# A three-layer graph network: attribute loads ten steps earlier, and early-row products in two PSUM banks

## Chip, core and metric

The kernel runs on one core of a Trainium2 chip. The metric is the device time of one execution in microseconds (us), the median of several runs. The engines are TensorE (PE, with its weight loads shown as PEld), VectorE (DVE), ScalarE (ACT), GpSimd (POOL) and the queue engine SyncE (SP). DMAs are issued from SP, ACT and POOL.

## What is computed

A relational graph convolution over 6250 nodes with 256 features and 100,000 edges with 32 attributes each, three layers deep, and a layer norm at the end. The edges come sorted by destination. Everything is float32.

```python
ew = edge_attr @ edge_w + edge_b                       # [100000, 256]
inv_cnt = [1 / max(segment_sum(edge_type == i, dst), 1) for i in range(3)]
x0 = x
for l in range(3):
    msg = relu(x[src] * ew)                            # gather of 100000 rows
    out = 0
    for i in range(3):
        h = segment_sum(msg * (edge_type == i), dst) * inv_cnt[i]
        out = out + h @ weights[l, i]
    x = x + relu(out + x @ roots[l] + biases[l])
return layernorm(x0 + x)
```

## The kernel before

**Pairs, quads and steps.** The edges are cut into 782 tiles of 128. Two tiles are a *pair* (391 of them, `U`), two pairs share one buffer `xs` and are called a *quad* here. Each layer walks over the pairs in an order written out by hand (`schedule`): first pairs 64 to 390, then 63 down to 0. So the edges of the lowest nodes, the first 128 rows above all, come last in a layer. The walk is a loop over steps `it`; in step `it` each kind of work handles the pair that lies some distance ahead or behind, and the instructions are issued in exactly this order on each engine (`manual_schedule`, no reordering).

**One quad's way through the engines.**
- POOL gathers its rows, four indirect DMAs of 128 rows (helper at L928), nine steps ahead of the reduction.
- PE multiplies the edge attributes by `edge_w` (`make_ew`, L623, PSUM tile `ew_p`, three banks, of which a quad takes two).
- DVE multiplies the two (`weigh`, two instructions, L645), ACT applies the relu (`bound`, L649), DVE makes one-hot matrices of the destinations (`one_hot`, L655).
- PE reduces the edges onto their destinations (`reduce`, L665, PSUM tile `h_p`), eight instructions to a pair in layers 1 and 2 and ten in layer 0. DVE adds the result into a ring `acc` (`add`, L683).

When all edges of a block of 128 nodes are in, `node_mul` (L711) and `node_end` (L742 to L745) finish the block's rows in `x_all`, and SP stores them to `x_mid[l]` in DRAM (L747), where the next layer gathers from. Block 0 is the last of a layer.

**The ring of row buffers.** `xs` has eight buffers (`ROWS`), three of which stay with the first three quads of layer 0 (`first_rows`, made ahead of the layers). Five rotate: the gathers of a quad wait until the quad five places before it has been reduced.

**Across a layer's end.** The first six pairs of the next layer, three quads, are gathered early (`gather_early`, L806), while block 0 isn't finished. In `x_mid` block 0 is zero until its store, so these quads lack what the first 128 rows contribute. `complete` (L634 to L639) puts it in: for each of a quad's two pairs PE multiplies `came`, a one-hot matrix of the sources below 128, with block 0 of `x_all`, and DVE adds the product to the pair's rows. The product of a pair fills the PSUM tile `o_p`, which has one bank (`o_pool`, `bufs=1`) and serves `node_mul` too. `r_p` (`r_pool`) is another tile of one bank; `root_turn` and `root_mul` use it (L688, L696) and, for blocks 0 and 1, the second half of `node_mul`. The store of block 0 waits for the twelve early gathers, which read `x_mid`; the gathers after them wait for that store.

**The attributes.** In layer 0 the attributes are loaded in their plain form (L536), turned by PE (L607), copied to the tile `at` by ACT (`keep_attrs`, L615) and kept in DRAM as `at_all` by SP (`store_at`, L599), eight pairs (512 KB) at a time. Layers 1 and 2 load `at` from there (`load_at`, L563). `at` has three buffers. The first two groups of the next layer are loaded by the layer before, at steps `U` and `U + 1` (`ats_next`), and handed on; the other loads come nine steps ahead of their use. In SP's queue these two loads stand behind the next layer's `r_sb` and `b_sb` (L552, L554, step `U - 10`). In layer 0 the last `store_at`, step `U - 5`, stands ahead of them too; the store of block 0 stands behind them.

Of the kernel before, what the change touches and what calls it, by code (L numbers as in the profile page):

```python
# [8 lines left out]
F32 = mybir.dt.float32  # L9
# [433 lines left out]
def ordered_path(ctx, tc, x, edge_attr, weights, roots, biases, edge_w, edge_b, out, src, src_i, seg, place_i, consts, rows,  # L443
# [7 lines left out]
    P = 128  # L451
    N, D = x.shape
    E, A = edge_attr.shape
    L, R = weights.shape[:2]
# [3 lines left out]
    U = T // 2  # L458
# [59 lines left out]
    o_pool = ctx.enter_context(tc.tile_pool(name="o_p", bufs=1, space=PSUM))  # L518
    r_pool = ctx.enter_context(tc.tile_pool(name="r_p", bufs=1, space=PSUM))

    groups = list(dict.fromkeys(u // 4 for u in order))
    at_groups = list(dict.fromkeys(u // GROUP for u in order))

    def first_of(p, n):
        return p == 0 or order[p - 1] // n != order[p] // n
# [4 lines left out]
    def load_attrs(g):  # L530

        an = ans[groups.index(g) % 3]
        t0 = 8 * g
        full = min(8, E // P - t0)
        if full > 0:
            nc.sync.dma_start(an.rearrange("p k i a -> p (k i) a")[:, :full, :A],  # L536
                              edge_attr[t0 * P:(t0 + full) * P, :].rearrange("(g p) a -> p g a", p=P))
        if 0 <= full < 8 and (t0 + full) * P < E:
            nc.sync.dma_start(an.rearrange("p k i a -> p (k i) a")[:E - (t0 + full) * P, full, :A],
                              edge_attr[(t0 + full) * P:, :])  # L540

    def load_x(c0):
        n = min(6, NT - 1 - c0)
        if n > 0:
            nc.scalar.dma_start(x_all[:, c0:c0 + n, :], x[c0 * P:(c0 + n) * P, :].rearrange("(c p) d -> p c d", p=P))
        if c0 + 6 >= NT - 1:
            last = N - (NT - 1) * P
            nc.scalar.dma_start(x_all[:last, NT - 1, :], x[N - last:, :])

    def load_root(l):  # L550
        r_sb = wpool.tile([P, DC, D], F32, name="r_sb")
        nc.sync.dma_start(r_sb, roots[l].rearrange("(c p) e -> p c e", p=P))  # L552
        b_sb = wpool.tile([P, D], F32, name="b_sb")
        nc.sync.dma_start(b_sb, biases[l:l + 1, :].to_broadcast([P, D]))  # L554
        return r_sb, b_sb

    def pairs_in(g):
        return min(GROUP, U - GROUP * g)

    def load_at(l, g):  # L560
        at = edge.tile([P, GROUP, P], F32, name="at", bufs=3)
        if l > 0:
            nc.sync.dma_start(at[:, :pairs_in(g)].rearrange("p k e -> p (k e)"), at_all[g, :, :pairs_in(g) * P])  # L563
        return at

    def find_came():
        e = 2 * P * order[0]
        nc.scalar.dma_start(came_i.rearrange("p t e -> p (t e)"),
                            src[e:e + 2 * FIRST * P][None, :].to_broadcast([P, 2 * FIRST * P]))
        for t in range(2 * FIRST):  # L570
            nc.vector.tensor_scalar(came[:, t, :], came_i[:, t, :], node_i[:, 0:1], None, op0=ALU.is_equal)

    def layer(l, r_sb, b_sb, ats, early, pools):
# [13 lines left out]
        r_next, ats_next, early_next = (None, None), {}, {}  # L587

        def gather(u):
            p = order.index(u)  # L590
            if p < FIRST:
                xs[u // 2] = early[u // 2]
            else:
                if first_of(p, 2):
                    xs[u // 2] = room(rows, D)
                gather_pair(nc, xs[u // 2], x_rows, src_i, u)
# [4 lines left out]
        def pairs_of(q):  # L601
            return range(min(2, U - 2 * q))
# [24 lines left out]
        def gather_early(p):  # L627
            u = order[p]
            if first_of(p, 2):
                early_next[u // 2] = room(rows, D)  # L630
            gather_pair(nc, early_next[u // 2], x_mid[l], src_i, u)

        def complete(q):
            for k in pairs_of(q):  # L634
                rest = o_pool.tile([P, 2, D], F32, name="o_p")
                for i in range(2):
                    nc.tensor.matmul(rest[:, i, :], came[:, 4 * q + 2 * k + i - 2 * order[0], :], x_all[:, 0, :],  # L637
                                     start=True, stop=True)
                nc.vector.tensor_add(xs[q][:, k], rest, xs[q][:, k])  # L639

        def weigh(q):
            n = len(pairs_of(q))
            for i in (1, 0):
                there = xs[q][:, :n, i, :]
                nc.vector.tensor_mul(there, ew_ps[q][i][:, :n, :], there)  # L645

        def bound(q):
            there = xs[q][:, :len(pairs_of(q))]
            nc.scalar.activation(there, there, AF.Relu)  # L649
# [116 lines left out]
        def load_x0(c):  # L766
            n = min(P, N - c * P)
            x0s[c] = edge.tile([P, D], F32, name="x0", bufs=2)
            if n < P:
                nc.vector.memset(x0s[c], 0.0)  # L770
            nc.sync.dma_start(x0s[c][:n, :], x[c * P:c * P + n, :])
# [12 lines left out]
        for it in range(-11, max(starts) + 7):  # L784
            def pair(k):
                return order[it + k] if 0 <= it + k < U else None
            if pair(AHEAD) is not None:
                gather(pair(AHEAD))
            if l < L - 1 and 0 <= it + AHEAD - U < FIRST:
                gather_early(it + AHEAD - U)  # L790
            if l == 0 and it == 20:
                find_came()
            if l == 0 and pair(11) is not None and first_of(it + 11, 4):
                load_attrs(pair(11) // 4)
            if l > 0 and pair(AHEAD) is not None and pair(AHEAD) // GROUP not in ats:
                ats[pair(AHEAD) // GROUP] = load_at(l, pair(AHEAD) // GROUP)
            if l == 0 and it >= -4 and (it + 4) % 20 == 0 and (it + 4) // 20 * 6 < NT - 1:
                load_x((it + 4) // 20 * 6)
            if it == 10:
                nc.sync.dma_start(w_sb, weights[l].rearrange("r (c p) e -> p (r c) e", p=P))  # L800
            if l == L - 1 and it + 2 in root_at:
                load_x0(root_at[it + 2])
            if l < L - 1 and it == U - 10:
                r_next = load_root(l + 1)
            if l < L - 1 and U <= it < U + 2:
                ats_next[at_groups[it - U]] = load_at(l + 1, at_groups[it - U])  # L806

            if pair(4) is not None and first_of(it + 4, 2):
                make_ew(pair(4) // 2)
            if pair(0) is not None:  # L810
                reduce(pair(0))
            if pair(-LAG) is not None:
                add(pair(-LAG))
            if pair(3) is not None and first_of(it + 3, 2):
                if l > 0 and it + 3 < FIRST:
                    complete(pair(3) // 2)
                weigh(pair(3) // 2)
                bound(pair(3) // 2)
            if l == 0:

                for k, work in ((6, keep_attrs), (7, turn)):
                    if pair(k) is not None and first_of(it + k, 2):
                        work(pair(k) // 2)
                if pair(4) is not None and last_of(it + 4, GROUP):
                    store_at(pair(4) // GROUP)
            if it in root_at:
                root_turn(root_at[it])
            if it - 1 in root_at:
                root_turned(root_at[it - 1])
            if it - 2 in root_at:  # L830
                root_mul(root_at[it - 2])
            if it - 3 in root_at:
                root_keep(root_at[it - 3])
            if it == moved:
                move()
            if it - 2 == moved:
                clear(P)
            if it + 1 in node_at and slot_of(node_at[it + 1]) == 0:
                wrap()
            if it in node_at:  # L840
                node_mul(node_at[it], 0)
            if it - 1 in node_at:
                node_end(node_at[it - 1], 0)
            if it - 2 in node_at:
                node_mul(node_at[it - 2], 1)
            if it - 3 in node_at:
                node_end(node_at[it - 3], 1)
                clear(slot_of(node_at[it - 3]))
            if it - 4 in node_at and l == L - 1:
                deviate(node_at[it - 4])  # L850
            if it - 5 in node_at and l == L - 1:
                norm(node_at[it - 5])
            if pair(2) is not None and first_of(it + 2, 2):
                one_hot(pair(2) // 2)
# [248 lines left out]
```

## Time and profile before

| | |
|---|---|
| median of 3 runs | 3021.46 us (3019.87 to 3021.53) |
| the profiled execution: its time, its span | 3018.21 us, 3016.4 us |
| PE busy | 2789.6 us, 92% of the span, mean granted clock 0.942 |
| POOL busy | 2236.2 us, 74% |
| DVE busy | 2080.6 us, 69% |
| ACT busy | 987.1 us, 33% |
| the products in `complete` (L637), four instructions to a pair | 1.10 to 1.16 us, 2.07 to 2.09 at half clock |
| the add in `complete` (L639) | 0.69 us |
| loads `at` from `at_all` | 96 of 512 KB |
| bytes moved | 438.87 MB, mean 145 GB/s |

Layer 0 ends near 1020 us (block 0 of `x_all` done at 1020.68), layer 1 near 2010 (2009.62). A share of busy time is a mean over the whole span; a matmul at half clock counts as busy for twice as long. A releaser named in brackets is inferred from the semaphores; "issue" stands for idle time whose end the profile can't put down to an instruction. In the chain of waits each line is a piece of the path that ended last, with its start and length.

### The profile page before, as it was taken

The page shows a single profiled execution, that of the slowest core. Times are in us where ns is not written, and L with a number is a line of the kernel's source. Part 1 is how long each engine was busy: PE and PEld are TensorE (multiplying, and loading weights), DVE is VectorE, ACT ScalarE, POOL GpSimd, SP SyncE. Part 2 cuts the span into 40 slices and gives each one's busy share as a digit, 9 for nine tenths or more (in the row PEclk, how much of TensorE's full clock was granted, in tenths as well). Part 3 has the DMA queues.
Part 4 walks back from the last instruction along what each step waited for, and adds up shares of the span by engine and source line. Part 5 has one row for each costly group of instructions (what it writes and reads, how often), then busy time and mean ns, then how long its engine had stood idle before and what let it go on. Part 6 is the DMA issues. An engine that isn't in the chain of part 4 may idle for free.

```text
span 3016.4 us, 55782 instructions
## 1 busy us (share of the span) xinstructions
PE 2789.6 (92%) x18114; PEld 2252.3 (75%) x18114; DVE 2080.6 (69%) x5865; ACT 987.1 (33%) x1354; POOL 2236.2 (74%) x2355
## 2 busy tenths in 40 slices
PE   6899999999999889999999999889999999999997
PEld 5777878888877667777777777667777777777775
DVE  6676767777776556666666667556667777877765
ACT  4444444444444222222222222212222222322221
POOL 6777777777777677777777777767777777777775
PEclk9999999999999899999999999878999999999888
DMA  5655555555555444444444445434554444444443
GB/s 154 176 162 161 166 165 151 149 158 156 159 156 145 144 125 137 139 132 140 134 142 144 144 137 149 151 116 140 151 149 146 147 147 149 142 144 144 135 139 97
DMA packets 274682, 438.87 MB, mean 145 GB/s; under 512 B 145004, under 2 KB 180032, under 8 KB 274384
## 3 DMA queue, kind: packets, MB, share of 16 engines
q0 software_dynamic: 112608, 307.65, 35.1%
q1 hardware_dynamic: 154720, 119.64, 13.4%
q10 hardware_dynamic: 7056, 7.92, 0.9%
q8 instruction: 149, 2.44, 0.3%
q14 instruction: 149, 1.22, 0.1%
HBM read 389.94 MB, written 45.09 MB: 144 GB/s over the span
## 4 chain that ended last, share of the span: by engine, by line
PE 56%; DMA 16%; POOL 10%; issue 8%; DVE 7%; ACT 2%; DVEq 0%; ACTq 0%; POOLq 0%; SPq 0%
PE h_p L665 25%; PE ew_p L623 16%; DMA xs<-x_mid,src_io 12%; POOL xs L928 10%; PE o_p L711 9%; DVE xs L645 4%; DMA xs<-in_x_dram,src_io 4%; PE r_p L696 3%; PE turn_p L607 1%; ACT xs L649 1%; DVE x_root L742 1%; DVE acc L683 1%; PE r_p L688 1%; PE o_p L637 0%; PE o_p L715 0%
## 5 line engine op out<-in xcount | busy, mean ns | idle before, releaser
L928 POOL DMA_INDIRECT xs<-x_mid,src_io x1564 | 1488.9, 952 | 503.5 <-issue 416.8
L665 PEld LDWEIGHTS h_p<-oh,xs 128*128 128x128 f32 x9384 | 1214.2, 204 | 245.9 <-issue 190.0
L665 PE MATMUL h_p<-oh,xs 128*128 128x120 f32 x9384 | 1346.3, 295 | 28.2 <-DVE acc L683 12.5
L649 ACT ACTIVATE xs<-xs 128x1024 f32<-128x1024 f32 x588 | 620.2, 1055 | 1857.3 <-DVE xs L645 1792.3
L645 DVE TENSOR_TENSOR xs<-ew_p,xs 128x512 f32<-128x512 f32 x1176 | 753.2, 682 | 558.1 <-DMA xs<-x_mid,src_io 362.0
L623 PE MATMUL ew_p<-ew_sb,at 33*128 33x256 f32 x4692 | 861.0, 418 | 151.3 <-DVE xs L645 149.2
L928 POOL DMA_INDIRECT xs<-in_x_dram,src_io x782 | 745.5, 953 | 255.3 <-issue 198.9
L623 PEld LDWEIGHTS ew_p<-ew_sb,at 33*128 33x128 f32 x4692 | 502.5, 191 | 393.8 <-DVE xs L645 192.1
L683 DVE TENSOR_TENSOR acc<-h_p,acc 128x240 f32 (+1 forms) x1173 | 517.7, 441 | 209.7 <-PE h_p L665 125.3
L655 DVE TENSOR_SCALAR oh<-iota_w,seg_o 128x120 f32<-128x120 f32 x2346 | 512.9, 293 | 0.0
L711 PE MATMUL o_p<-w_sb,acc 128*128 128x256 f32 (+1 forms) x1716 | 442.4, 395 | 4.9 <-DVE acc L683 4.9
L711 PEld LDWEIGHTS o_p<-w_sb,acc 128*128 128x128 f32 (+1 forms) x1716 | 319.1, 198 | 41.7 <-DVE acc L683 6.3
L742 DVE SCALAR_TENSOR_TENSOR x_root<-o_p,inv,x_root 128x256 f32<-128x256 f32 (+1 forms) x429 | 205.7, 480 | 47.0 <-PE o_p L711 39.4
L696 PE MATMUL r_p<-r_sb,t_s 128*128 128x256 f32 x588 | 160.7, 397 | 0.1
L659 ACT ACTIVATE oh_b<-oh 128x480 bf16<-128x480 f32 x196 | 117.9, 602 | 101.3 <-DVE oh L655 99.6
L728 ACT ACTIVATE acc<-zero_o 128x768 f32<-128x768 f32 (+1 forms) x150 | 140.5, 937 | 29.1 <-PE r_p L711 19.1
L696 PEld LDWEIGHTS r_p<-r_sb,t_s 128*128 128x128 f32 x588 | 106.6, 202 | 9.2 <-ACT t_s L692 0.3
L665 PE MATMUL h_p<-oh_b,full_ones 128*128 128x120 bf16 x782 | 107.5, 220 | 0.0
L607 PE MATMUL turn_p<-ident_o,an 128*128 128x128 f32 x391 | 79.4, 286 | 10.7 <-DMA an<-in_edge_attr_dram 6.1
L665 PEld LDWEIGHTS <-full_ones 128*128 128x128 bf16 x782 | 81.9, 105 | 2.5
L699 DVE TENSOR_TENSOR x_root<-r_p,b_sb 128x256 f32<-128x256 f32 x147 | 61.1, 416 | 24.0 <-PE r_p L696 19.5
L615 ACT ACTIVATE at<-turn_p 128x256 f32<-128x256 f32 x196 | 71.7, 366 | 2.7 <-PE turn_p L607 2.7
(93 smaller groups left out, 526.6 us busy)
## 6 DMA issues: line engine op xcount, KB each, us to landing
at<-at_all SPq DMA_DIRECT2D x96, 512.0 KB
xs<-x_mid,src_io POOLq DMA_INDIRECT x1564
at_all<-at SPq DMA_DIRECT2D x48, 512.0 KB
xs<-in_x_dram,src_io POOLq DMA_INDIRECT x782
an<-in_edge_attr_dram SPq DMA_DIRECT2D x97, 128.0 KB
x_mid<-x_all SPq DMA_DIRECT2D x96, 128.0 KB
x_all<-in_x_dram ACTq DMA_DIRECT2D x8, 768.0 KB
x<-in_x_dram SPq DMA_DIRECT2D x48, 128.0 KB
```

The source lines that it names most:

```text
L623: nc.tensor.matmul(ew_ps[q][i][:, k, :], ats[2 * q // GROUP][i * UP:i * UP + A1, (2 * q + k) % GROUP, :], ew_sb[i * UP:i * UP + A1, :], st ...
L645: nc.vector.tensor_mul(there, ew_ps[q][i][:, :n, :], there)
L649: nc.scalar.activation(there, there, AF.Relu)
L655: nc.vector.tensor_scalar(ohs[q][:, t, :], iota_w, seg[:, 4 * q + t:4 * q + t + 1], None, op0=ALU.is_equal)
L659: nc.scalar.activation(oh_bs[q][:, :n], ohs[q][:, :n], AF.Copy)
L665: nc.tensor.matmul(h_ps[u][:, d, :], xs[u // 2][:, u % 2, i, d * P:(d + 1) * P] if d < DC else full_ones, (ohs if d < DC else oh_bs)[u // ...
L683: nc.vector.tensor_tensor(there, h_ps[u][:, :CH].rearrange("p c (r w) -> p c r w", r=R), there, op=ALU.add)
L696: nc.tensor.matmul(rs[c][:, 1, :], t_ss[c][:, d, :], r_sb[:, d, :], start=(d == 0), stop=(d == DC - 1))
L711: nc.tensor.matmul(o_p[:n, j, :], acc[:, d, r, slot:slot + n], w_sb[:, r * DC + d, :], start=(d == 0), stop=(d == DC - 1))
L728: nc.scalar.activation(acc[:, :CH, :, slot:slot + P], zero[:, :, None, None].to_broadcast([P, CH, R, P]), AF.Copy)
L742: nc.vector.scalar_tensor_tensor(root, o_p[:n, j, :], inv[:n, c, r:r + 1], root, op0=ALU.mult, op1=ALU.add)
L928: nc.gpsimd.indirect_dma_start(out=xs[:, u % 2, i, :], out_offset=None, in_=x_rows[:, :], in_offset=bass.IndirectOffsetOnAxis(ap=src_i[:, ...
```

## The change

Two edits. In `complete`, the product of a quad's second pair goes to a tile of `r_pool` in place of `o_pool`. The loads of the next layer's first two groups of attributes are issued at steps `U - 10` and `U - 9` in place of `U` and `U + 1`. An added empty line moves the numbers of all lines from 635 on by one in the changed kernel.

```diff
         def complete(q):
             for k in pairs_of(q):
-                rest = o_pool.tile([P, 2, D], F32, name="o_p")
+
+                rest = (r_pool if k else o_pool).tile([P, 2, D], F32, name="r_p" if k else "o_p")
                 for i in range(2):
                     nc.tensor.matmul(rest[:, i, :], came[:, 4 * q + 2 * k + i - 2 * order[0], :], x_all[:, 0, :],
                                      start=True, stop=True)
...
             if l < L - 1 and it == U - 10:
                 r_next = load_root(l + 1)
-            if l < L - 1 and U <= it < U + 2:
-                ats_next[at_groups[it - U]] = load_at(l + 1, at_groups[it - U])
+            if l < L - 1 and U - 10 <= it < U - 8:
+                ats_next[at_groups[it - U + 10]] = load_at(l + 1, at_groups[it - U + 10])
```

The order of the instructions on POOL, ACT, PE and DVE is the same as before; on PE and DVE some of them name the other tile. On SP the order differs in one place, at the end of layer 0: the two loads stand ahead of the last store of `at_all` there.

## Prediction

> **What bounds the kernel now.** I read the page's table of groups first, then the busy time of each engine over stretches cut where the layers meet, then the timeline of POOL there, and last the chain of waits in the two places where POOL stands still.
>
> ```profile
> L928 POOL DMA_INDIRECT xs<-x_mid,src_io x1564 | 1488.9, 952 | 503.5 <-issue 416.8
> ```
>
> ```profile
> 1046.00:2013.00 967.00, 893.49 (x5523) 715.95 (x5520) 626.01 (x1794) 255.49 (x298) 732.61 (x770) 0.94 0.46 138
> 2041.00:2996.00 955.00, 885.09 (x5455) 709.17 (x5456) 687.22 (x2015) 266.23 (x344) 722.09 (x758) 0.93 0.48 144
> ```
>
> (Columns of the two stretches: length, busy time of PE, PEld, DVE, ACT and POOL with their instructions, granted clock, DMA share, GB/s.) PE is 92% busy, yet it isn't the bound of layers 1 and 2. A gather takes 0.95 us on POOL and the next starts 0.30 us later, so 1.25 us each. 770 gathers in the first stretch are 962.5 us of its 967, and 758 are 947.5 of 955. Inside a layer POOL never rests, and PE's slack takes up what PE loses. Only where POOL stands still is there time to win. That is at the two layer changes (start, length, engine, line; in brackets the idle time before it and its releaser):
>
> ```profile
> 1017.23 0.95 POOL L928 DMA_INDIRECT xs<-x_mid,src_io  x1 [0.30 <-issue]
> 1023.17 0.94 POOL L928 DMA_INDIRECT xs<-x_mid,src_io  x1 [5.00 <-DMA x_mid<-x_all]
> ...
> 1038.50 0.95 POOL L928 DMA_INDIRECT xs<-x_mid,src_io  x1 [5.61 <-issue]
> ...
> 1045.92 1.00 POOL L928 DMA_INDIRECT xs<-x_mid,src_io  x1 [2.71 <-issue]
> ```
>
> ```profile
> 2017.28 0.94 POOL L928 DMA_INDIRECT xs<-x_mid,src_io  x1 [4.31 <-DMA x_mid<-x_all]
> ...
> 2029.28 0.94 POOL L928 DMA_INDIRECT xs<-x_mid,src_io  x1 [2.27 <-issue]
> ...
> 2041.19 0.94 POOL L928 DMA_INDIRECT xs<-x_mid,src_io  x1 [7.21 <-issue]
> ```
>
> The first stop of each change is the store of the first 128 rows (x_mid) and its landing. The other two are marked "issue", but the program has POOL wait there until the first, then the second quad of the new layer has been reduced, so that its xs buffer is free. The trace agrees: reductions end at 1037.76 and 1045.17, POOL goes on 0.74 and 0.75 us later. After 1045.92 and 2041.19 POOL runs without a stop. So **the start of the seventh quad's gathers (1045.92 and 2041.19) is what the change must move**; all later work of layers 1 and 2 moves with it. PE sets it, by this chain (first change):
>
> ```profile
> 1020.81 1.12 PE o_p L637 x4
> 1021.93 0.02 issue
> 1021.95 0.70 DVE xs L639
> 1022.66 0.04 issue
> 1022.70 1.15 PE o_p L637 x4
> ```
>
> Products of one pair, the add on DVE, then the products of the next pair: they share the one bank o_p, so PE waits for the add.
>
> **Step 1, two banks.** The instructions are the same in number, size and order on PE and DVE. The second product of a quad goes to r_p, which was last read before x_all's first rows were done, and for that the first product waits anyway. So the wait in the middle goes: 0.02 + 0.70 + 0.04, with rounding 0.77 us (1021.93 to 1022.70; again 1027.64 to 1028.41 and 1038.67 to 1039.44). The first add then lies beside the second products (0.70 under 1.13); late next is the second add, which the weighing needs. Three quads: 3 x 0.77 = 2.3 us at each change, **4.6 us** for two. New waits: quad 1's second product waits for quad 0's second add, but weighing and the attribute products stand in between and are later. Root_turn's transposes use r_p next, after the weighing of quad 2, which is again past that add: nothing. PE alone would queue behind these waits.
>
> **Step 2, the attributes.** The order of SP's queue changes at the first change of layers only: there the two loads (512 KB each) pass the last store of at_all. At the second, no instruction lies between old place and new, and SP issued them at 1957 and 1977 already, 30 us before they were needed: nothing. PE never waited for these loads at either change: the first attribute product (1019.10) has "issue" before it. What the loads do cost now is bandwidth:
>
> ```profile
> 999.74 0.34 SPq L599 DMA_DIRECT2D at_all<-at  x1
> 1000.18 1.21 SPq L563 DMA_DIRECT2D at<-at_all  x2
> ```
>
> ```profile
> 1002.22 6.13 DMA xs<-in_x_dram,src_io
> ```
>
> Store and loads, 1.5 MB, are in the DMA engines (0.90 busy from 1000 to 1005) when layer 0's last gather is issued. It takes 6.13 us; DVE waits 4.09 us for it and PE sits idle 4.35 us. Moved, the first load goes out behind b_sb's (978.60 + 0.83, about 979.5), the second when PE has made the fifth-last quad's weights and so left its buffer (about 984). Then only the store is beside the last gather. Not in the trace; the nearest row is the gather of 977.20, with a store and 384 KB of roots and biases beside it: 4.39 us. A free one takes 2.8. I take 4.39, which brings the end of layer 0 forward by **1.7 us**; bounds 3.3 (6.13 - 2.8) and -0.7. The latter is the collision moved: gathers near 980 to 987 land up to 3.3 us later, and the slow clock there (0.50 from 983 to 993) takes one more window. Then PE, which was idle from 1005.9, ends the quad before last up to 5.0 us later, at 1010.9, where it now starts the last one at 1010.23. SP holds nothing else between 984 and 999.7, so its wait for PE delays nobody. The x_mid store, queued behind, must still wait for the twelfth early gather (1017.23 + 2.8 = 1020.0, the store was at 1020.70), so POOL restarts only 0.6 us sooner; but the chain above starts 1.7 sooner.
>
> **Step 3, the clock, which no edit names.** At both changes the granted clock falls to half:
>
> ```profile
> 2010.00:2015.00 5.00, 3.28 (x14) 1.98 (x13) 2.85 (x6) 0.10 (x1) 2.35 (x3) 0.89 0.34 100
> 2015.00:2020.00 5.00, 4.16 (x12) 2.42 (x9) 1.28 (x5) 0.96 (x1) 2.11 (x3) 0.50 0.68 210
> ```
>
> In quarter-microsecond stretches it was 0.50 from 1027.5 to 1037.5, and from 2014.0 to 2041.0. At half clock four product instructions take 2.08 us, not 1.13; six of the attribute products 2.07, not 1.13; a quad's reduction 3.70, not 1.98. The first change pays about 3.6 us for that (one of each on the chain), the second about 10 (four, three and two). The Trainium skill, "TensorE: Matmul & The Clock Gate", Part 1, says that the clock falls after an idle window of some 3.4 us and comes back after a busy one, the windows running free. The row differs: it fell at 2013.8 though PE had been busy for 81% of the 13.5 us before, with no gap over 0.9 us in the last five, and PE's unbroken run from 2022.77 to 2030.26 did not bring it back. Taken literally the rule has no slow stretch here, and a sum of 6.3 us. The spacing of the changes (1997.0, 2000.25, 2014.0, 2041.25) does fit multiples of 3.4 us, so I keep the window and drop the limit.
> With two banks the unbroken run at the second change grows: attributes, reduction, four products (2.07 + 3.77 + 4.15 = 10 us, now 7.5). I estimate that it brings the clock back a window or two sooner: one attribute group and one reduction at full clock, 0.94 + 1.72 = **2.7 us**. Bounds: the clock never falls, and POOL's own rate sets the end (rival 2), or the first change becomes as slow as the second, -6.4 (10 - 3.6). Near the middle, since the gap that goes makes PE busier, not idler. Two sections of the same page speak against the edit: cycling through PSUM banks left PE micro-idle and its clock swinging ("A second HAM failure mode: psum-queue depth-cycling"), and double-buffered PSUM brought another kernel no further gain ("HAM oscillation"). Here the row has the idle time inside the one-bank form, 0.77 us thrice; by the rule step 1 would be worth 0 to -6.4, by the row +2.3 per change. I follow the row.
>
> **Sum.** 4.6 + 1.7 + 2.7 = 9.0 us. Against the profiled execution's 3018.2 (span 3016.4 and 1.8 around it): 3009.2. That execution lies 3.3 us, 0.1%, below the median of the runs, 3021.46; from the median the time is **3012.5**.
>
> **Rivals.**
> 1. *The clock falls earlier at the first change and stays down* (slower). Place: 1020 to 1046. For: with a shorter cycle, a 3.4 us window may hold mostly attribute products and the add-and-weigh gap, as at 2010.5 to 2014, when it fell. Against: busy share rises. Price: 6.4 at the first change, and the moved loads bring -0.7 besides: 6.4 + 0.7 - 4.6 = 2.5 slower, 3024. It decides from 4.6 us of extra slow work on.
> 2. *POOL's stream takes over.* The clock holds, PE frees the buffers in time, and POOL runs from its restart. First change: 1022.5 + 12 x 1.25 = 1037.5, not 1045.92, 8.4 won; second: 2017.28 + 15 = 2032.3, not 2041.19, 8.9 won. Together 17.3: 3004. For: the chain at full clock would have the second quad reduced some 19 us after x_all (2009.62), at 2029. Against: the add-and-weigh gap of 0.9 us or more per quad stays.
> 3. *The loads were hidden and the clock does what it did.* Only step 1: 4.6, 3017. For: PE was idle before the last gather, so a later lag may eat what the earlier landing gives.
> That the change doesn't do what it says is true of step 2 at the second change and is in the sum.
>
> **How the numbers follow.** Forecast, 6 to 12 us won, 0.45; rival 2, 0.20; rival 3, 0.25; rival 1, 0.10. A measurement tells 0.2%, 6.0 us, from no change. Faster by more: forecast, rival 2 and a little of rival 3, 0.70. Within: rival 3 and most of rival 1, 0.24. Slower by more, where rival 1 meets a worse collision: 0.06. The range runs from rival 2's 3004 to 3019, past rival 3 with half of its gain lost.
>
> **What would show it.** Step 1: no DVE row between the two product groups of a quad, eight L637 matmuls in a row. Step 2: the loads at about 979 and 984, and under 4.5 us for layer 0's last gather. Step 3: less than 27 us at 0.50 in the second change. In all: the waits of POOL before the sixth and seventh quads' gathers, 8.3 us at the first change and 9.5 at the second, must shrink, and nothing between the changes may. It is wrong if they stay, or if POOL stops anew after them.

## The result, and the profile after

The changed kernel takes 3005.17 us (median of 7 runs, 3001.44 to 3012.53) where the kernel before takes 3021.46 (7 runs, 3015.11 to 3024.66): ratio 0.9951, interval 0.9937 to 0.9965. The medians lie 16.3 us apart; by the ratio, which is estimated from all runs, it is 14.8 us less (10.6 to 19.0). Gains below are worked out from such ratios. The profiled execution took 3001.44 us with a span of 2999.6, 16.8 below the span before. In the changed kernel the products are at L638, the add at L640, the gathers at L929.

The table of groups first:

```profile
L929 POOL DMA_INDIRECT xs<-x_mid,src_io x1564 | 1486.4, 950 | 486.9 <-issue 398.4
```

The gathers' idle time (behind the second bar) went from 503.5 us to 486.9: 16.6 of the 16.8. The stretches inside the two layers (length, busy time and instructions of PE, PEld, DVE, ACT and POOL, granted clock, DMA share, GB/s):

```profile
1046.00:2004.00 958.00, 890.43 (x5470) 712.10 (x5468) 619.61 (x1777) 253.09 (x295) 725.28 (x765) 0.94 0.47 138
2041.00:2980.00 939.00, 867.91 (x5336) 695.63 (x5336) 676.91 (x1981) 261.06 (x337) 708.03 (x745) 0.93 0.48 143
```

765 gathers in 958.0 us and 745 in 939.0 are 1.252 and 1.260 us each, as before (1.256 and 1.260). So nothing changed inside the layers, and the time came from the changes between them. POOL's timeline there (start, length, and in brackets the idle time before it and its releaser), first change, then second. In each the rows are the twelfth early gather, the *restart* (the next gather, behind the store of block 0), and the first gathers of the sixth and of the seventh quad:

```profile
1017.87 0.95 POOL L929 DMA_INDIRECT xs<-x_mid,src_io  x1 [0.30 <-issue]
1023.19 0.95 POOL L929 DMA_INDIRECT xs<-x_mid,src_io  x1 [4.38 <-PE o_p L638]
...
1033.26 0.95 POOL L929 DMA_INDIRECT xs<-x_mid,src_io  x1 [0.30 <-issue]
...
1039.19 1.03 POOL L929 DMA_INDIRECT xs<-x_mid,src_io  x1 [1.23 <-issue]
```

```profile
2003.66 0.95 POOL L929 DMA_INDIRECT xs<-x_mid,src_io  x1 [0.30 <-issue]
2008.95 0.94 POOL L929 DMA_INDIRECT xs<-x_mid,src_io  x1 [4.35 <-PE r_p L638]
...
2019.00 0.94 POOL L929 DMA_INDIRECT xs<-x_mid,src_io  x1 [0.30 <-issue]
...
2023.99 0.94 POOL L929 DMA_INDIRECT xs<-x_mid,src_io  x1 [0.30 <-PE h_p L666]
```

POOL's first stop, before its restart, stays: 4.38 us at the first change, 5.00 before, and 4.35 at the second, 4.31 before. (The product that is printed as its releaser is not what ended it: the store of block 0 left at 1020.72 and 2006.49, and POOL went on 2.5 us later each time.) The stop before the sixth quad's gathers is gone at both changes; that before the seventh's is 1.23 us at the first change and gone at the second. From the restart to the seventh quad's gathers it is now 16.00 and 15.04 us, not 22.75 and 23.91: 6.75 + 8.87 = 15.6 us of the 16.8. Twelve gathers at 1.25 us are 15.0, so at the second change POOL runs at its own rate.

The edit itself shows in the timeline at the second change:

```profile
2002.13 1.13 PE L638 MATMUL o_p<-x_all,came 128*128 128x256 f32 x4 [0.49 <-DVE x_all L746]
...
2003.09 1.03 PE L638 MATMUL r_p<-x_all,came 128*128 128x256 f32 x4
2003.35 0.69 DVE L640 TENSOR_TENSOR xs<-o_p,xs 128x512 f32<-128x512 f32 x1 [1.28 <-PE o_p L638]
...
2004.16 0.69 DVE L640 TENSOR_TENSOR xs<-r_p,xs 128x512 f32<-128x512 f32 x1
```

Eight products follow one another without a wait, and the first add (2003.35) lies beside the second four. The clock there, in stretches of 5 us (columns as above):

```profile
2005.00:2010.00 5.00, 3.65 (x16) 2.43 (x16) 3.81 (x9) 1.06 (x1) 0.94 (x1) 1.00 0.48 138
2010.00:2015.00 5.00, 4.66 (x24) 4.24 (x25) 1.63 (x6) 1.06 (x1) 3.84 (x4) 0.69 0.54 175
2015.00:2020.00 5.00, 4.03 (x21) 2.77 (x20) 3.82 (x10) 1.06 (x1) 3.77 (x4) 0.97 0.37 106
```

It still falls, but for 3.25 us (2012.0 to 2015.25 in quarter-microsecond stretches), not 27. At the first change it is at half for 10.0 us (1022.25 to 1032.25), as long as before.

The moved loads, in SP's queue and the timeline at the end of layer 0:

```profile
980.03 4.46 SPq L563 DMA_DIRECT2D at<-at_all  x2
998.99 0.32 SPq L599 DMA_DIRECT2D at_all<-at  x1
```

```profile
1002.85 0.95 POOL L929 DMA_INDIRECT xs<-in_x_dram,src_io  x1 [0.30 <-issue]
1005.69 1.29 DVE L646 TENSOR_TENSOR xs<-ew_p,xs 128x512 f32<-128x512 f32 x2 [1.31 <-DMA xs<-in_x_dram,src_io]
```

Both loads are out by 984.5, and only the store is left beside layer 0's last gather. The gather now takes 2.84 us from its issue to the weighing (1002.85 to 1005.69), not 6.23 (1002.22 to 1008.45, of which the prediction's row shows 6.13), and DVE waits 1.31 us for it, not 4.09.

### The profile page after: what moved, and what is told of

Same layout as the page of the kernel before. It is cut to its first block, busy times and chain, and to the rows that moved or that the text cites. A ratio compares the mean times of both kernels' runs of the same rounds, so it can differ in the third digit from the quotient of the medians.

```text
span 2999.6 us, 55787 instructions
## 1 busy us (share of the span) xinstructions
PE 2780.4 (93%) x18114; PEld 2246.6 (75%) x18114; DVE 2083.0 (69%) x5865; ACT 986.7 (33%) x1354; POOL 2232.3 (74%) x2355
## 3 DMA queue, kind: packets, MB, share of 16 engines
q1 hardware_dynamic: 154720, 119.64, 13.5%
## 5 line engine op out<-in xcount | busy, mean ns | idle before, releaser
L929 POOL DMA_INDIRECT xs<-x_mid,src_io x1564 | 1486.4, 950 | 486.9 <-issue 398.4
L929 POOL DMA_INDIRECT xs<-in_x_dram,src_io x782 | 744.1, 952 | 257.3 <-issue 207.3
L712 PE MATMUL o_p<-w_sb,acc 128*128 128x256 f32 (+1 forms) x1716 | 435.1, 391 | 3.9 <-DVE acc L684 3.9
```

What stands on the lines that cost most here:

```text
L712: nc.tensor.matmul(o_p[:n, j, :], acc[:, d, r, slot:slot + n], w_sb[:, r * DC + d, :], start=(d == 0), stop=(d == DC - 1))
L929: nc.gpsimd.indirect_dma_start(out=xs[:, u % 2, i, :], out_offset=None, in_=x_rows[:, :], in_offset=bass.IndirectOffsetOnAxis(ap=src_i[:, ...
```

## The experiments

The theory after the result: the second bank shortens PE's chain at each change, directly and by a higher clock, until POOL's own rate takes over; the loads bring little. The rivals: the loads did it; the clock did it and the overlap is a trifle; or POOL's buffers are the real limit, and any relief there is worth as much. Times are against the kernel before, run on the same chip (3014.39 us for the first four experiments, 3014.2 for the two after them, 3015.89 for the last two).

### The two banks alone

```diff
-                rest = o_pool.tile([P, 2, D], F32, name="o_p")
+                rest = (r_pool if k else o_pool).tile([P, 2, D], F32, name="r_p" if k else "o_p")
```

> The kernel before with the second product of a quad in r_p; the loads stay at the layer's end. Theory A (two edits, two places: the banks act at both layer changes, the loads only through layer 0's last gather): block 0 is done near 1020.7 as before, the seventh quad's gathers come 2.3 us sooner at the first change (near 1043.6) and 8 to 9 us sooner at the second, where POOL's own rate then sets the pace; about 10.5 us won, 3011. Theory B (the banks do all of it, the loads were hidden anyway): 15 to 16 us, 3005. Theory C (only the wait for the add goes, the clock stays as it was): 4.6 us, 3017.

3000.95 us, ratio 0.996 (0.9945 to 0.9974), 12.1 us less (7.8 to 16.6). That excludes theory C's 4.6; the time can't tell A's 10.5 from B's 15 to 16. Its profiled execution was a long one (3011.85 us, with a layer 0 that ended late, which the edit doesn't touch), but its changes of layers show the same as the whole change's:

```profile
1028.81 0.95 POOL L928 DMA_INDIRECT xs<-x_mid,src_io  x1 [4.95 <-PE r_p L637]
...
1044.94 1.03 POOL L928 DMA_INDIRECT xs<-x_mid,src_io  x1 [1.37 <-issue]
...
2017.14 0.94 POOL L928 DMA_INDIRECT xs<-x_mid,src_io  x1 [4.33 <-DMA x_mid<-x_all]
...
2032.16 0.97 POOL L928 DMA_INDIRECT xs<-x_mid,src_io  x1 [0.30 <-issue]
```

16.13 and 15.02 us from restart to seventh quad. The clock was full through both. The second bank carries most of the change at least.

### The early loads alone

```diff
-            if l < L - 1 and U <= it < U + 2:
-                ats_next[at_groups[it - U]] = load_at(l + 1, at_groups[it - U])
+            if l < L - 1 and U - 10 <= it < U - 8:
+                ats_next[at_groups[it - U + 10]] = load_at(l + 1, at_groups[it - U + 10])
```

> The kernel before with the two attribute loads ten steps earlier; one PSUM bank. Theory A: layer 0's last gather lands in under 3 us in place of 6.1, block 0 is done 4 us sooner (near 1016.5), the seventh quad's gathers 4 us sooner at the first change, nothing at the second: 4 us won, 3017. Theory B: 3021, no change. If the first change's slow-clock stretch falls elsewhere, 1 to 4 us either way.

3014.65 us, ratio 0.9996 (0.9984 to 1.0009): between 4.8 us less and 2.7 more. The gain of 4 us that one theory expected lies near the edge of that interval, and the prediction's 1.7 well inside it. The last gather of layer 0 was quick here too (2.91 us to its weighing, 1003.55 to 1006.46), but POOL still stops twice after its restart at the first change:

```profile
1018.64 0.95 POOL L928 DMA_INDIRECT xs<-x_mid,src_io  x1 [0.30 <-issue]
1023.99 0.95 POOL L928 DMA_INDIRECT xs<-x_mid,src_io  x1 [4.40 <-ACT xs L649]
...
1036.72 0.94 POOL L928 DMA_INDIRECT xs<-x_mid,src_io  x1 [2.95 <-issue]
...
1044.11 1.00 POOL L928 DMA_INDIRECT xs<-x_mid,src_io  x1 [2.70 <-issue]
```

In the kernel before, block 0's store left at 1020.70, as soon as block 0 was done (1020.67). Here block 0 was done sooner, at 1017.22, but the store then waited for the twelfth early gather (1018.64) and left at 1021.51. So POOL restarts 5.35 us after that gather, not 5.94: of an earlier end of layer 0, little reaches the restart.

### All eight row buffers rotate

Instead of three buffers that stay with layer 0's first quads and five that rotate, eight fixed buffers are handed out in turn. The kernel before is otherwise unchanged; one bank, loads late.

```diff
+import itertools
...
-    return rows.tile([128, 2, 2, D], F32, name="xs", bufs=ROWS)
+    return next(rows)
...
-    rows = ctx.enter_context(tc.tile_pool(name="rows", bufs=ROWS))
+    rows_pool = ctx.enter_context(tc.tile_pool(name="rows", bufs=1))
+    rows = itertools.cycle([rows_pool.tile([128, 2, 2, D], F32, name=f"xs{i}") for i in range(ROWS)])
```

> The kernel before with all eight row buffers rotating in place of five: no edit of PE's work, of the banks or of the loads. If POOL's wait for a reduced quad is what carried PE's delay into the layer (theory A), POOL runs from its restart without a stop at both changes, the seventh quad's gathers come 15 us after the restart in place of 22.8 and 23.9, and 15 to 17 us are won, 3005, though PE's products still wait for the add and the clock still falls. If the time is PE's own and not POOL's (rival), 3021.

2992.37 us, ratio 0.9926 (0.9912 to 0.9940), 22.3 us less, where 15 to 17 were expected. POOL and clock at the second change:

```profile
2002.49 0.94 POOL L929 DMA_INDIRECT xs<-x_mid,src_io  x1 [4.34 <-DMA x_mid<-x_all]
...
2016.25 0.95 POOL L929 DMA_INDIRECT xs<-x_mid,src_io  x1 [0.30 <-PE o_p L638]
2017.50 0.95 POOL L929 DMA_INDIRECT xs<-x_mid,src_io  x1 [0.30 <-issue]
```

```profile
2000.00:2005.00 5.00, 4.16 (x12) 2.43 (x9) 1.40 (x5) 1.06 (x1) 1.91 (x3) 0.50 0.63 202
2005.00:2010.00 5.00, 4.64 (x13) 2.35 (x11) 2.74 (x7) 1.06 (x1) 3.78 (x5) 0.50 0.38 112
```

The clock is at half, the products wait for the add as before, PE's chain is as long as before (24.90 and 26.94 us from block 0 done to the second quad reduced), and yet POOL runs through in 15.04 and 15.01 us. So a slow PE alone costs nothing between the restart and the seventh quad; it costs where POOL must wait for a buffer that PE frees. The third rival holds in this sense: at the changes of layers, what the second bank gains is an end to that wait. What goes beyond the forecast comes from layer 0, where the kernel before stops for buffers as well: 6.42 us before the gather of 57.41 and 2.64 before that of 94.84. These two stops are gone with eight buffers, and POOL passes the first layer's gathers in 983.2 us, not 991.3 (start of the first to start of the last).

### One product more, read by nobody

After the products of each pair, one product of the same kind into a tile that nothing reads. Products still wait for the add; only PE has less idle time.

```diff
+                spare = r_pool.tile([P, 2, D], F32, name="r_p")
+                nc.tensor.matmul(spare[:, 0, :], came[:, 4 * q + 2 * k - 2 * order[0], :], x_all[:, 0, :],
+                                 start=True, stop=True)
```

> The kernel before with one more 128x128x256 product after each pair's two, into r_p, read by nobody: one bank for what is used, the waits for the adds stay, but PE has work in the gap (two instructions, 0.55 us, in a wait of 0.77). If the second change's gain comes from the clock (step 3), it stays up longer there: less than 14 us at half in place of 27, 4 to 8 us won, 3013 to 3017. If it comes from the overlap of product and add alone, nothing is won: 3021 to 3024, more where the clock is at half and the filler takes 1.1 us.

3003.48 us, ratio 0.9967 (0.9953 to 0.9981), 10 us less (5.7 to 14.2), more than the 4 to 8 expected, though the interval reaches into them. Timeline and clock at the second change:

```profile
2007.39 1.13 PE L637 MATMUL o_p<-x_all,came 128*128 128x256 f32 x4 [0.49 <-DVE x_all L748]
...
2008.35 0.59 PE L640 MATMUL r_p<-x_all,came 128*128 128x256 f32 x2
...
2009.36 1.13 PE L637 MATMUL o_p<-x_all,came 128*128 128x256 f32 x4 [0.41 <-DVE xs L642]
```

```profile
2010.00:2015.00 5.00, 4.17 (x19) 2.49 (x17) 3.52 (x8) 1.06 (x1) 2.24 (x3) 1.00 0.66 210
2015.00:2020.00 5.00, 4.52 (x25) 3.31 (x26) 2.74 (x7) 1.06 (x1) 3.78 (x5) 1.00 0.37 105
```

The second four products still start behind the add, the clock stays at 1.00, and the chain to the second quad reduced is 20.84 and 20.89 us, not 24.50 and 30.84. So the slow clock cost that chain about 3.7 and 10.0 us, and more work for PE makes the kernel faster. From restart to seventh quad it took 17.28 and 16.81 us. That the clock stays up with the filler in every execution isn't shown: one was profiled; the time is of six.

### Ring and store: what is left

The changed kernel with eight rotating buffers (the ring's diff above), and the same with block 0 kept apart: the early gathers read `x_mid` as before, the others a second copy to which every block is stored, so that block 0's store needn't wait for the early gathers.

```diff
+    x_full = [dram.tile([N, D], F32, name=f"x_full{l}") for l in range(L - 1)]
...
-        x_rows = x if l == 0 else x_mid[l - 1]
+        x_rows = x if l == 0 else x_full[l - 1]
...
-                nc.sync.dma_start(x_mid[l][c * P:c * P + n, :], x_all[:n, c, :])
+                nc.sync.dma_start(x_full[l][c * P:c * P + n, :], x_all[:n, c, :])
+                if c > 0:
+                    nc.sync.dma_start(x_mid[l][c * P:c * P + n, :], x_all[:n, c, :])
```

> The changed kernel with all eight row buffers rotating. Theory A (the change won its time by taking PE's delay off POOL's buffer wait): with eight buffers there is nothing left to take off, so the two gains don't add; 22 to 23 us below the kernel before, as the eight buffers alone (ratio 0.9926), with 15 us from restart to the seventh quad's gathers at both changes. If the gains add (rival: PE's chain itself is the bound), 36 us, ratio 0.988.

> The changed kernel with all eight row buffers rotating, and each block but the first stored twice: the early gathers read x_mid as before, the others read a second copy that also gets block 0. So block 0's store no longer waits for the twelfth early gather. If POOL's stream sets the time and its stop at the store is all that is left of the layer change (theory A), the stop of 5.3 us between the twelfth early gather and the next shrinks to under 2 us at both changes: 7 us less than with the eight buffers alone; against the kernel before 27 to 30 us, ratio near 0.990. Against it stand 96 further stores of 128 KB (12.6 MB, 3%) beside the gathers: if these slow the stream, no gain over the eight buffers alone.

The changed kernel with the ring: 2991.45 us, ratio 0.9922 (0.9909 to 0.9936). The ring alone gave 0.9926: on top of it the change brings nothing that can be measured, and POOL takes 15.0 and 15.1 us from restart to seventh quad. With the second copy too: **2986.57 us**, 0.9908 (0.9892 to 0.9923), 27.7 us less and the fastest kernel of the study, though its interval overlaps that of the ring. Its restarts:

```profile
1007.23 0.95 POOL L933 DMA_INDIRECT xs<-x_mid,src_io  x1 [0.30 <-issue]
1009.05 0.94 POOL L933 DMA_INDIRECT xs<-x_full,src_io  x1 [0.87 <-PE r_p L640]
...
1990.54 0.95 POOL L933 DMA_INDIRECT xs<-x_mid,src_io  x1 [0.30 <-issue]
1995.10 0.94 POOL L933 DMA_INDIRECT xs<-x_full,src_io  x1 [3.61 <-PE r_p L640]
```

From the twelfth early gather to the restart it is 1.82 us at the first change, but 4.56 at the second, where less than 2 was expected. There block 0 isn't done until 1992.34, and the store and its landing take the rest: the early gathers were only one of two conditions.

### Both kernels again

One more profile of each, and then the second bank alone and the whole change timed on one chip.

> The kernel before, unchanged, profiled once more. If the half-clock stretch at the layer changes depends on how free-running windows fall, the time from POOL's restart to the seventh quad's gathers differs from the first profile's 22.8 and 23.9 us by some us in either place, between 17 (clock up throughout, with three waits of 0.77 us) and 25. If it is fixed by the program, 22.8 and 23.9 again.

> The changed kernel, unchanged, profiled once more. With two banks the same interval should be near POOL's floor of 15.0 us at least at one of the changes, and never above 20; if the first profile was luck, 20 to 24.

> The banks alone once more, timed beside the whole change on one chip. If the loads add nothing on top of the banks (with two banks POOL's rate already sets the pace from its restart, and the restart hangs on the twelfth early gather), both come out within 3 us of each other, each 11 to 16 us below the kernel before.

> The whole change, timed beside the banks alone. Within 3 us of them if the loads add nothing; 4 us or more below them if the earlier end of layer 0 reaches the end of the program (ratio lower by 0.0014 or more).

Before again: span 3020.4, restart to seventh quad 20.01 and 25.03 us. After again: span 2996.1, 15.06 and 15.01. Timed: second bank alone 3003.12, ratio 0.9962 (0.9949 to 0.9976); whole change 3001.86, 0.9957 (0.9944 to 0.9971). The loads' share is lost in the intervals. The profiled execution of the whole change in this timing, its third profile (3014.61 us), goes against the expectation that it would never take over 20 us from restart to seventh quad. At its first change POOL stopped as often as with one bank:

```profile
1026.72 0.94 POOL L929 DMA_INDIRECT xs<-x_mid,src_io  x1 [4.51 <-PE r_p L638]
...
1039.94 0.94 POOL L929 DMA_INDIRECT xs<-x_mid,src_io  x1 [3.53 <-issue]
...
1046.94 1.01 POOL L929 DMA_INDIRECT xs<-x_mid,src_io  x1 [2.32 <-issue]
```

That is 20.22 us. Two things met: the clock was at half for 10 us (from 1030.25), and block 0 was done only 2.5 us before the restart. One sum shows how these go together.

### One sum for all profiles

POOL takes the seventh quad's buffer when the second quad is reduced, 0.75 us after the reduction's end. So the time from restart to seventh quad should be PE's **chain** (from the end of `x_all`'s block 0 to the end of the second quad's reduction) plus 0.75, less PE's **head start** (from block 0 done to POOL's restart), and never under POOL's own 15.0. It holds for the kernels in which five buffers rotate. For the first change of the changed kernel these rows carry it:

```profile
1016.03 0.43 DVE L746 SCALAR_TENSOR_TENSOR x_all<-x_root,x_all 128x256 f32<-128x256 f32 x1
...
1036.40 2.04 PE L666 MATMUL h_p<-oh,xs 128*128 128x120 f32 x16
```

Chain 1016.46 to 1038.44, 21.98 us; head start 1016.46 to 1023.19, 6.73; 21.98 + 0.75 - 6.73 = 16.00, and 16.00 was measured. The same sum for the others, in us:

| kernel, change | clock at half in the chain | chain | head start | sum | measured |
|---|---|---|---|---|---|
| before, first | 10.0 | 24.50 | 2.50 | 22.75 | 22.75 |
| before, second | 26.4 | 30.84 | 7.67 | 23.92 | 23.91 |
| before again, first | 10.0 | 24.62 | 5.35 | 20.02 | 20.01 |
| before again, second | 18.4 | 27.76 | 3.47 | 25.04 | 25.03 |
| loads alone, first | 13.5 | 26.14 | 6.77 | 20.12 | 20.12 |
| loads alone, second | 10.0 | 24.81 | 6.05 | 19.51 | 19.50 |
| filler, second | 0 | 20.89 | 4.82 | 16.82 | 16.81 |
| banks alone, first | 0 | 17.88 | 2.50 | 16.13 | 16.13 |
| banks alone, second | 0 | 17.76 | 7.76 | 15.0 (10.75) | 15.02 |
| whole change, second | 3.25 | 19.39 | 6.88 | 15.0 (13.26) | 15.04 |
| whole change, third profile, first | 10.0 | 21.98 | 2.51 | 20.22 | 20.22 |

The six changes of the same kernels that the table leaves out come within 0.1 us of the sum too. Three things can be read off. At the same 10 us of half clock the chain is 24.50 to 24.81 with one bank and 21.98 with two: the overlap alone is worth 2.7 us. With two banks a microsecond at half clock costs 0.4 ((21.98 - 17.88) / 10). And the head start, 2.5 to 7.8 us, differs from execution to execution as much as the chain does. What sets it stands in the same profiles: block 0's store leaves as soon as block 0 is done, or some 2.8 us after the twelfth early gather's start, whichever is later, and POOL restarts 2.5 us after the store leaves. So the head start is 2.5 us where block 0 comes last, as in the third profile, and longer where it is done early.

## Why the prediction was nearly right, step by step

The time lies within the range and its sign was right, but 7.3 us below the forecast, and the mechanism that the profile shows is that of **rival 2**: POOL's stream takes over. The forecast's gain of 9.0 us lies outside the measured interval of 10.6 to 19.0, the 17.3 of rival 2 inside it. The range reached down to 3004 because that rival was priced into it; the sum of the three steps alone did not reach the measured gain. Rival 2 had the seventh quad at restart + 15.0 at both changes. The first profile shows 16.00 at the first change and 15.04 at the second, 15.6 us won in all. In timed runs it is 14.8 (10.6 to 19.0); one execution at least, the third profile, kept its stops at the first change.

- **What bounds the kernel**: held. The rate inside the layers is as it was, and 15.6 of the profile's 16.8 us came from the time between restart and seventh quad.
- **Step 1, 0.77 us three times a change, 2.3**: the mechanism held, the three waits are gone. Measured at equal clock, 2.7 a change. The page "TensorE: Matmul & The Clock Gate" of the Trainium skill, in "A second HAM failure mode: psum-queue depth-cycling", tells of another kernel in which cycling through PSUM banks left PE idle for short times and its clock swinging. Here it is the other way round. Over the changes of all profiles the chain had a mean of 14.2 us at half clock with one bank (8 changes, each 10 or more, the filler's left out) and 4.4 with two (14 changes, 10 at most). The row was the better guide, since it showed that the idle time sat in the one-bank form.
- **Step 2, the last gather at 4.39 us, 1.7 won**: the gather came down further, to 2.84, near its other bound, and PE's idle time of 4.35 us before the last quad's reduction fell to 1.57. The loads went out at 980 and 984, as the step had it. But what arrives at the program's end can't be told from nothing: 1.2 us less alone, between 4.8 less and 2.7 more. A gather that lands sooner lets block 0 end sooner, and that lengthens PE's head start; but the head start at the first change was 2.5 to 5.5 us with the loads late and 2.5 to 6.8 with them early, a spread between executions that is larger than the step's 1.7. With two banks, moreover, a longer head start meets POOL's floor.
- **Step 3, the clock, 2.7**: **this is the term that was mis-sized.** The mean chain is 26.3 us with one bank and 19.8 with two, 6.5 less a change. Of this 2.7 is overlap, so the clock's part is 3.8 a change, 7.6 for both, where the sum had 2.7. (It agrees with 14.2 - 4.4 = 9.8 us less at half clock, at 0.4 each.) The step gave the first change nothing and let the clock come back a window or two sooner at the second. The prices of the slow clock that it used, 3.6 and 10, were right (the filler: 3.7 and 10.0); what was wrong was how much of the slow clock would go. The forecast was read from one execution's stretch of 27 us, which was the longest at any change; with two banks the chain had 0 to 10.
- **The sum.** Overlap and clock offer 2 x 6.5 = 13.0 us. The mean time from restart to seventh quad fell by 4.3 and 7.8, 12.0 together (three profiles with one bank, five with two), as far as POOL's floor allows; the second bank alone was timed at 12.1 and 11.5. The prediction held its sum and POOL's floor apart as rivals, though both act in one execution: the gain of 9.0 was too small because of the clock's term, and the cap, which its forecast left out, kept the rest from showing in full.
- **Rival 1**, the clock falls earlier and stays down: at the first change it did fall earlier in the changed kernel (1022.25, not 1027.5), but for the same 10 us and never for longer. **Rival 3**, only the overlap: out, as 12 us are more than 4.6 and the filler shows what the clock is worth.

In the profiles, the filler's gain goes with a clock that stays up (one profile), and so does the clock's part of the banks' gain (seven). Why the clock stays up is not shown. Both make PE busier in the wait for the add, but both also write the bank `r_p` there, and no run keeps the two apart.

## What to carry to other kernels

Before pricing a wait on a busy engine, find which resource it holds up (here a row buffer) and what the next limit's floor is (here twelve gathers); gains at such a wait draw on the same few microseconds above that floor. Here those of the change and of more buffers didn't add. A stop that two edits attack may be cured by a third that touches neither: eight rotating buffers instead of five won 22 us with PE as slow as ever. And where a clock differs from one execution to the next, take its stretch from several profiles before it goes into a sum.

## What the runs showed of the hardware that was not expected

- How long the clock stays at half in a change of layers differs from one execution of the same program to the next. The stretches lie near multiples of 3.4 us (1, 3, 5 and 8 times 3.4 are 3.4, 10.2, 17.0 and 27.2). Read in quarter-microsecond stretches they were, in the profiles of the kernel before, 10.0 and 27 us (first and second change), then 10.0 and 17; in those of the changed kernel 10.0 and 3.25, then 3.25 and two of some 3, then 10.0 and 3.
- Giving TensorE useless products made the kernel 10 us faster (ratio 0.9967, 0.9953 to 0.9981).
- Two profiles of the whole change, by the same program, had 16.00 and 20.22 us at the first change with the same chain of 21.98: the head start alone, 6.73 and 2.51 us, made the difference.
